# Left operands of seven feed forward units: transposed by TensorE, or made as rows and transposed by DMA

## The chip, the cores and the metric

The kernel runs on one core of one Trainium2 chip. The metric is the device time of one execution in microseconds. Before the change three runs gave 2137.55, 2141.11 and 2142.48 us, a median of 2141.11.

A core has TensorE (PE, the matrix engine), VectorE (DVE), ScalarE (ACT), GpSimd (POOL) and SyncE (SP), each with its own instruction stream that it runs in order. In this kernel SP issues nearly all transfers between the chip's memory and the on-chip SBUF; 16 DMA engines carry them. TensorE writes to PSUM, from where DVE and ACT read.

## The reference

One transformer-like block over x of shape (4, 1024, 2048), taken as 4096 rows of 2048:

```
mod = (silu(c) @ wmod).reshape(4, 6, 1, 2048)
sa, ca, ga, sb, cb, gb = mod[:, 0], ..., mod[:, 5]      # ga and gb are kept at least 0.25 from zero
h = layernorm(x) * (1 + ca) + sa
x = x + ga * (long convolution of h along 2048 + D[0] * h)
h = layernorm(x) * (1 + cb) + sb
x = x + gb * (h @ W.T + bias + sum_e w_e * (h @ A_e.T) @ B_e.T)      # w = coeffs * scales, 16 adapters
```

The change bears on the last two lines, the feed forward part: a modulated layer norm of x, and a 2048 x 2048 matrix product with the adapters merged into W.

## The kernel before

**Stages.** First come the modulation products (L317), the tables of the convolution, then 32 blocks of 128 rows through the convolution (`conv_mm`, L614), with the merging of the adapters into W between them (`merge`, L486 to L533). The result of a block, with the residual added, is written to memory as `x1d` (L656), and its mean and scale are kept in `ln2`. Then comes the feed forward part.

**Feed forward.** It works on 16 units of 256 rows (`NU`), and goes over them twice: pass q = 0 makes one half of the output columns, q = 1 the other (the loop at L1079 to L1108). A unit is a 2 x 2 block product by Strassen's scheme (Winograd's form): seven products in place of eight, in the order `ORDER = (0, 4, 5, 1, 6, 2, 3)`. Every operand is held as two half precision numbers, a high part and the remainder (`hl`), and a product takes three matmuls for each of eight chunks: 24 matmuls of 128x128 by 128x512 (`prod`, L750). ACT copies some products out of PSUM (L758), DVE combines them with the residual and the gate (L768 to L802), SP stores the output (L775). The PSUM banks X, Y and Z of a unit are each accumulated onto again later in the same unit: product 6 adds to the bank of product 5, product 1 to that of 0, product 2 to that of 4, product 3 to that of 6.

**Weights.** `load_w` (L980) loads the right operand of one product, 2 x 1 MB, and keeps it for a whole pass in `wc`. At the change of pass each is loaded anew, once the last unit's product has used the old one.

**Left operands.** `left` (L683) makes the seven left operands of a unit. It loads two 128x2048 tiles of `x1d`, normalizes them with ACT (L690), transposes them on TensorE, 32 transposes of 128x128 float32 per unit (L700), and ACT applies `cb` and `sb`, which in that layout are one number per partition, while it empties PSUM (L702). Then come the sums and differences of Strassen's scheme on DVE (L719 to L726), and for each operand `put`: ACT makes the high part (L712), DVE the remainder (L713), SP stores the pair to `lfd` (L714). In pass 0 the operand is used from SBUF where it was made; in pass 1 `left_load` (L731) brings it back from `lfd`. The pool `l` that holds the operands has 8 buffers, one operand of 512 KB each.

**What sets the order.** `left` is a generator. The function `tick` (L1098) is called after each product of a unit u and takes steps of the generator of unit u + 1 as `LPLAN` tells: the transposes come in groups of eight behind the first four products, then the sums, then the loads for unit u + 2. The recording layer orders each engine's stream by its own estimate of when things are ready, starting from the program's order, and puts in the waits. A transfer has one of eight completion semaphores in turn, so an SP transfer also waits until the eighth one before it has landed. Residual tiles `xo` come from the pool `o`, five buffers for four tiles per unit.

Of the kernel before, what the change touches and what calls it, by code (L numbers as in the profile page):

```python
# [12 lines left out]
F32 = mybir.dt.float32  # L13
F16 = mybir.dt.float16
# [5 lines left out]
MUL, ADD, SUB = ALU.mult, ALU.add, ALU.subtract  # L20
# [4 lines left out]
P = 128  # L25
D = 2048
# [8 lines left out]
class Net:  # L35
# [644 lines left out]

    def left(self, pl, u, res):  # L683
        nc, v = self.nc, self.nc.vector
        b = u // 4
        xs = []
        for r in range(2):
            x = pl["x2"].tile([P, D], F32, tag=f"x2{r}", name="x2")
            nc.sync.dma_start(out=x, in_=self.x1d[2 * u + r])
            nc.scalar.activation(  # L690
                x, x, AF.Identity, bias=self.ln2[:, 2 * u + r, 0:1], scale=self.ln2[:, 2 * u + r, 1:2]
            )
            xs.append(x)
        yield
        t = pl["t"].tile([P, NC, 2, P], F32, tag="t", name="gt")
        for c0 in range(0, NC, 2):
            tp = self.tps.tile([P, 2, 2, P], F32, tag="t", name="tp2")
            for c in range(2):
                for r in range(2):
                    nc.tensor.transpose(tp[:, c, r], xs[r][:, ds(P * (c0 + c), P)], self.ident)  # L700
            for c in range(2):
                nc.scalar.activation(  # L702
                    t[:, c0 + c], tp[:, c], AF.Identity,
                    bias=self.sb[:, c0 + c, b : b + 1], scale=self.cb[:, c0 + c, b : b + 1],
                )
            yield
        a11, a12 = t[:, 0:HC, 0, :], t[:, HC:NC, 0, :]
        a21, a22 = t[:, 0:HC, 1, :], t[:, HC:NC, 1, :]

        def put(i, s):  # L710
            hl = pl["l"].tile([P, HC, 2, P], F16, tag="l", name="lf")
            nc.scalar.copy(hl[:, :, 0, :], s)  # L712
            v.tensor_tensor(hl[:, :, 1, :], s, hl[:, :, 0, :], SUB)  # L713
            STQ(nc).dma_start(out=self.lfd[u, i], in_=hl)  # L714
            res[i] = hl

        put(0, a11)
        s = pl["s"].tile([P, HC, P], F32, tag="s", name="s")
        v.tensor_tensor(s, a21, a22, ADD)  # L719
        put(4, s)  # L720
        v.tensor_tensor(s, s, a11, SUB)
        put(5, s)
        put(1, a12)
        v.tensor_tensor(a21, a11, a21, SUB)
        put(6, a21)
        v.tensor_tensor(s, a12, s, SUB)  # L726
        put(2, s)
        put(3, a22)
        yield

    def left_load(self, pl, u, i):  # L731
        hl = pl["l"].tile([P, HC, 2, P], F16, tag="l", name="lf")
        self.nc.sync.dma_start(out=hl, in_=self.lfd[u, i])
        return hl

    def left_again(self, pl, u):
        return {i: self.left_load(pl, u, i) for i in ORDER}

    def ffn_unit(self, pl, u, q, lf, wc, tick):
        nc, v = self.nc, self.nc.vector  # L740
        ps = {}

        def prod(i, name):
            first = name not in ps
            if first:
                ps[name] = self.acc.tile([P, 512], F32, tag="a", name="f" + name)
            n = 0
            for k in range(HC):
                for x, y in ((0, 0), (0, 1), (1, 0)):
                    nc.tensor.matmul(  # L750
                        ps[name], lf[i][:, k, x, :], wc[i][k // 4][:, k % 4, y, :],
                        start=(first and n == 0), stop=(n == 3 * HC - 1), skip_group_check=True,
                    )
                    n += 1

        def copy(name, tag):
            t = pl["e"].tile([P, 512], F32, tag=tag, name=tag)
            nc.scalar.copy(t, ps[name])  # L758
            return t

        def at(x, r, h):
            return x[ds(P * r, P), ds(1024 * h + 512 * q, 512)]

        xs = {}
        for r, h in ((0, 0), (1, 1), (0, 1), (1, 0)):
            x = pl["o"].tile([P, 512], F32, tag="o", name="xo")
            nc.sync.dma_start(out=x, in_=at(self.x1d[2 * u : 2 * u + 2].rearrange("r p d -> (r p) d"), r, h))
            v.tensor_tensor(x, x, self.gbias[:, h], ADD)  # L768
            xs[r, h] = x

        def finish(r, h, cv, t):
            x = xs[r, h]
            v.tensor_tensor(t, cv, self.gbt[:, h], MUL)  # L773
            v.tensor_tensor(x, x, t, ADD)
            STQ(nc).dma_start(out=at(self.io["out"][ds(256 * u, 256), :], r, h), in_=x)  # L775


        prod(0, "X")
        p1 = copy("X", "p1")
        tick()  # L780
        prod(4, "Y")
        p5 = copy("Y", "p5")
        tick()
        prod(5, "Z")
        p6 = copy("Z", "p6")
        tick()
        prod(1, "X")
        finish(0, 0, ps["X"], pl["e"].tile([P, 512], F32, tag="p7", name="fin"))
        v.tensor_tensor(p6, p6, p1, ADD)
        tick()  # L790
        prod(6, "Z")
        p7 = copy("Z", "p7")
        v.tensor_tensor(p5, p5, p1, ADD)
        v.tensor_tensor(p7, p7, p5, ADD)
        finish(1, 1, p7, p7)
        tick()
        prod(2, "Y")
        v.tensor_tensor(p6, p6, ps["Y"], ADD)
        finish(0, 1, p6, p6)
        tick()  # L800
        prod(3, "Z")
        v.tensor_tensor(p1, p1, ps["Z"], ADD)  # L802
        finish(1, 0, p1, p1)
        tick()
# [5 lines left out]
MR = 2  # L810
ACC, TPS = 5, 2
PLAN = ("PNSL", "NL", "NSL", "NTL", "SL", "SL", "SL", "SL", "FSL", "SSL")
LPLAN = ("LL", "LL", "LL", "LL", "L", "0", "")
R0 = 5
WM, WMS = 3, 3
ROWC = 2700
# [7 lines left out]
def STQ(nc):  # L824
    return nc.sync
# [7 lines left out]
def net(ctx: ExitStack, tc: tile.TileContext, io):  # L833
# [3 lines left out]
    make_identity(nc, k.ident)  # L837
    k.x1d = k.dram.tile([32, P, D], F32, tag="x1d", name="x1d")
    k.ln2 = k.const("ln2", [P, 32, 2])
    k.lfd = k.dram.tile([NU, 7, P, HC, 2, P], F16, tag="lfd", name="lfd")  # L840

    def pool(stack, name, bufs, side="left"):
        return stack.enter_context(tc.tile_pool(name=name, bufs=bufs, side=side, reuse_waits="tile"))
# [37 lines left out]
    def take(g, n):  # L881
        for _ in range(n):
            next(g, None)
# [76 lines left out]
    def rest():  # L960
        mods = (x for sec in (4, 3, 5) for x in section(sec, (wmp,)))
        n = 0
        for _ in mer:
            yield
            n += 1
            if n % MR == 0:
                next(mods, None)
                yield
        for _ in mods:
            yield  # L970
        k.ginv = k.fold_scale(msm, k.cb, k.sb, "fs2", k.winv)
        yield

    fill = rest()
# [16 lines left out]

    def early():
        right.close()
        for name, bufs in (("w", 1), ("l", 8), ("t", 1), ("s", 1), ("x2", 1)):
            pr[name] = pool(p2, "p2" + name, bufs, "right")
        load_w(0, ORDER[0])

    def next_left(u):
        if u >= NU:
            return iter(())  # L1000
        lf[u] = {}
        return k.left(pr, u, lf[u])

    calls = [0]

# [63 lines left out]
        post = (r, xs.pop(r), *y)  # L1069
        nxt = follow[0] if follow else iter(())  # L1070
    k.conv_post(pl, *post)
    take(lgen, 10)
    gens = [next_left(1)]
    take(gens[0], 1)
    left.close()

    for name in ("v", "o", "e", "g"):
        pr[name] = pool(p2l, "p2" + name, 5 if name == "o" else 1)
    for q in range(2):  # L1079
        for i in ORDER:  # L1080
            if i not in wc or q == 1:
                load_w(q, i)
            if q == 1:
                lf.setdefault(0, {})[i] = k.left_load(pr, 0, i)
        for u in range(NU):
            b = u // 4
            if u % 4 == 0:
                ts_ = []
                for i in range(2):
                    t = pr["g"].tile([P, 2, 512], F32, tag=f"gb{i}", name=f"gb{i}")  # L1090
                    src = k.gbd[i][b].rearrange("(h n) -> h n", h=2)[:, ds(512 * q, 512)]
                    nc.sync.dma_start(out=t, in_=src.partition_broadcast(P))
                    ts_.append(t)
                k.gbt, k.gbias = ts_
                nc.vector.tensor_scalar(k.gbt, k.gbt, k.ginv[:, b : b + 1], None, MUL)
            plan = iter(LPLAN)

            def tick():  # L1098
                if q == 1:
                    return  # L1100
                for a in next(plan):
                    if a == "0":
                        gens[0] = next_left(u + 2)
                    take(gens[0], 1)

            k.ffn_unit(pr, u, q, lf.pop(u), wc, tick)
            if q == 1 and u + 1 < NU:
                lf[u + 1] = k.left_again(pr, u + 1)  # L1108
    p2l.close()
    p2.close()  # L1110

# [55 lines left out]
```

## Time and profile before

| what | value |
|---|---|
| median of three runs | 2141.11 us |
| the profiled execution | 2141.87 us |
| its span | 2140.1 us, mean granted TensorE clock 0.988 |
| first feed forward matmul | 918.9 us |
| last transpose of L700 | 1502.1 us |
| last feed forward matmul starts | 2134.2 us |
| moved by the DMA engines | 484.11 MB |
| products, L750 | 5376 matmuls, mean 379 ns of one (overlapping) |
| transposes, L700 | 512, mean 274 ns of one (overlapping) |
| PSUM to SBUF with cb and sb, L702 on ACT | 256, mean 576 ns |
| remainder of an operand, L713 on DVE | 112, mean 1219 ns |
| sum of two halves, L719 on DVE | 16, mean 1225 ns |
| residual plus bias, L768 on DVE | 128, mean 690 ns |

The page of a profile tells, for one execution, each engine's busy time and a picture of the span in 40 slices (a digit is the busy share in tenths). Behind it stand views that the trace answers: groups of instructions by line, who waited for whom, the instructions in order of time, and the busy time of all engines in a chosen stretch. Durations of matmuls and transposes overlap: the time that one costs is read from the distance between starts. The profile is of one execution, so sums made from it are set against that execution's own 2141.87 us.

### The profile page before, as it was taken

To read this page: it belongs to the slowest core of one execution; us is meant where nothing else is said; L and a number is where in the kernel's file an instruction comes from. 1 tells how busy PE (TensorE), PEld (TensorE's weight loads), DVE (VectorE), ACT (ScalarE), POOL (GpSimd) and SP (SyncE) were. 2 spreads that over 40 slices of the span, in tenths; PEclk is the share of its full clock that TensorE was granted. 3 is DMA by queue.
4 is the path that set the end of the run, shared out by engine and by line. 5 is a ranking of instruction groups with operands and counts; after the bars stand their busy time and mean duration, and the time that the engine had idled before them with its cause. 6 is when DMAs were issued, how large, how long until landed. Compare 5 with 4: busy or idle time off the path is not lost.

```text
span 2140.1 us, 28438 instructions
## 1 busy us (share of the span) xinstructions
PE 2082.4 (97%) x11113; PEld 1026.1 (48%) x11113; DVE 1308.4 (61%) x2353; ACT 923.7 (43%) x1695; POOL 6.3 (0%) x18
## 2 busy tenths in 40 slices
PE   7898999999999999999999999999999999999998
PEld 2344455555555555554545545555444444444444
DVE  5439898898979999665565565575533323332323
ACT  1325876677767777745454555555200000000000
POOL 0000000000000000000000000000000000000000
PEclk7999999999999999999999999999999999999999
DMA  9977566787776554387564564564794645454542
GB/s 401 373 307 278 225 227 265 285 310 262 276 278 227 187 192 173 139 346 258 190 241 180 202 240 179 203 235 172 283 341 163 192 151 167 164 170 165 177 157 69
DMA packets 127236, 484.11 MB, mean 226 GB/s; under 512 B 13608, under 2 KB 13768, under 8 KB 95998
## 3 DMA queue, kind: packets, MB, share of 16 engines
q1 hardware_dynamic: 126192, 477.55, 61.4%
q10 hardware_dynamic: 526, 2.63, 0.4%
q8 instruction: 87, 1.43, 0.3%
q0 software_dynamic: 384, 2.11, 0.2%
q14 instruction: 47, 0.39, 0.0%
HBM read 326.94 MB, written 155.30 MB: 225 GB/s over the span
## 4 chain that ended last, share of the span: by engine, by line
PE 67%; DVE 18%; ACT 6%; DMA 5%; issue 2%; SPq 0%; ACTq 0%; POOL 0%; DVEq 0%; POOLq 0%
PE fZ L750 22%; PE fY L750 15%; PE fX L750 15%; PE ya L614 5%; PE yb L614 3%; PE tp L700 3%; DVE wch L514 2%; PE modps L317 2%; DVE st L540 2%; DVE hc L593 2%; DVE y L641 2%; ACT x L660 2%; DMA wcd<-wch 1%; ACT t L582 1%; PE lps L486 1%
## 5 line engine op out<-in xcount | busy, mean ns | idle before, releaser
L750 PEld LDWEIGHTS <-lf 128*128 128x128 f16 x5376 | 526.0, 98 | 620.9 <-issue 1.4
L750 PE MATMUL fZ<-w,lf 128*128 128x512 f16 x2304 | 513.6, 379 | 0.8 <-ACT p L758 0.8
L750 PE MATMUL fX<-w,lf 128*128 128x512 f16 x1536 | 342.8, 379 | 0.0
L750 PE MATMUL fY<-w,lf 128*128 128x512 f16 x1536 | 342.0, 379 | 0.0
L614 PEld LDWEIGHTS <-hc 128*128 128x128 f16 x2304 | 215.3, 98 | 204.6 <-issue 41.6
L768 DVE TENSOR_TENSOR xo<-xo,gb 128x512 f32<-128x512 f32 x128 | 87.8, 690 | 238.7 <-DMA xo<-x1d 227.2
L582 ACT ACTIVATE t<-tp,sa,ca 128x128 f32<-128x128 f32 x480 | 188.1, 471 | 21.6 <-PE tp L578 12.9
L614 PE MATMUL ya<-kh,hs 128*128 128x512 f16 (+3 forms) x768 | 193.7, 326 | 3.7 <-DVE kh L284 2.6
L614 PE MATMUL ya<-kh,hc 128*128 128x512 f16 (+3 forms) x768 | 192.7, 328 | 3.8 <-ACT qs L627 3.6
L614 PE MATMUL yb<-kh,hc 128*128 128x512 f16 (+3 forms) x768 | 192.2, 327 | 1.8 <-DVE y L640 1.4
L758 ACT COPY p<-fZ 128x512 f32<-128x512 f32 x64 | 37.2, 581 | 286.8 <-PE fZ L750 272.1
L614 PEld LDWEIGHTS <-hs 128*128 128x128 f16 x1152 | 105.9, 98 | 108.6 <-issue 28.4
L758 ACT COPY p<-fX 128x512 f32<-128x512 f32 x32 | 18.7, 585 | 316.3 <-PE fX L750 210.4
L702 ACT ACTIVATE gt<-tp,sb,cb 128x256 f32<-128x256 f32 x256 | 124.9, 576 | 60.8 <-PE tp L700 60.8
L317 PE MATMUL modps<-wm,sct 128*32 128x512 f32 x768 | 118.8, 662 | 14.1 <-DMA wm<-in_wmod 14.1
L614 PE MATMUL ya<-kl,hc 128*128 128x512 f16 (+3 forms) x384 | 125.8, 328 | 0.0
L614 PE MATMUL ya<-kl,hs 128*128 128x512 f16 (+3 forms) x384 | 125.1, 326 | 0.7 <-DVE kl L285 0.7
L614 PE MATMUL yb<-kl,hc 128*128 128x512 f16 (+3 forms) x384 | 125.6, 327 | 0.0
L773 DVE TENSOR_TENSOR fin<-fX,gb 128x512 f32<-128x512 f32 x32 | 22.1, 692 | 128.4 <-PE fX L750 128.3
L593 DVE TENSOR_TENSOR hc<-t,hc 128x512 f16<-128x512 f32 x128 | 87.5, 684 | 6.6 <-ACT hc L592 6.4
L486 PE MATMUL lps<-lbh,lac 128*128 128x512 f16 x256 | 86.3, 379 | 1.2 <-DVE we L488 1.2
L578 PE MATMUL tp<-ident,n 128*128 128x128 f32 x512 | 79.3, 280 | 8.1 <-ACT t L582 6.3
(264 smaller groups left out, 2228.0 us busy)
## 6 DMA issues: line engine op xcount, KB each, us to landing
wm<-in_wmod SPq DMA_DIRECT2D x96, 1024.0 KB
lfd<-lf SPq DMA_DIRECT2D x112, 512.0 KB
lf<-lfd SPq DMA_DIRECT2D x112, 512.0 KB
x<-in_x SPq DMA_DIRECT2D x32, 1024.0 KB
x1d<-y SPq DMA_DIRECT2D x32, 1024.0 KB
x<-x1d SPq DMA_DIRECT2D x32, 1024.0 KB
xo<-x1d SPq DMA_DIRECT2D x128, 256.0 KB
out<-xo SPq DMA_DIRECT2D x128, 256.0 KB
```

The source lines that it names most:

```text
L317: self.last = self.nc.tensor.matmul(self.modps[32 * g : 32 * g + 32, :], self.sct[:, j].rearrange("p r b -> p (r b)"), w[:, ds(512 * g, 512)],
L486: nc.tensor.matmul(ps, la[:, x, k, h], y[:, k, osl], start=(n == 0), stop=(n == 5))
L514: v.tensor_tensor(hl[:, :, 1, :], tv, hl[:, :, 0, :], SUB)
L578: nc.tensor.transpose(tp[:, k], n[:, ds(P * (c0 + k), P)], self.ident)
L582: nc.scalar.activation(t[:, k], tp[:, k], AF.Identity, bias=self.sa[:, c, b : b + 1], scale=self.ca[:, c, b : b + 1],)
L593: v.tensor_tensor(lo[:, sl], src, hi[:, sl], SUB)
L614: nc.tensor.matmul(pf[:, o:512], h, self.kf[f][z][:, ds(k0, 512 - o)], start=first, stop=(i == last and (x, z) == (1, 0)), skip_group_chec ...
L700: nc.tensor.transpose(tp[:, c, r], xs[r][:, ds(P * (c0 + c), P)], self.ident)
L702: nc.scalar.activation(t[:, c0 + c], tp[:, c], AF.Identity, bias=self.sb[:, c0 + c, b : b + 1], scale=self.cb[:, c0 + c, b : b + 1],)
L750: nc.tensor.matmul(ps[name], lf[i][:, k, x, :], wc[i][k // 4][:, k % 4, y, :], start=(first and n == 0), stop=(n == 3 * HC - 1), skip_grou ...
L758: nc.scalar.copy(t, ps[name])
L768: v.tensor_tensor(x, x, self.gbias[:, h], ADD)
```

## The change

Units 2, 4, 6 to 14 (`BYDMA`) get another way to their left operands. `left_dma` normalizes the two tiles with ACT as before, and multiplies and adds the modulation on DVE while the rows are still rows; for this `mod_rows` writes `cb` and `sb` to memory as rows (`cbd`), and they come back broadcast over the 128 partitions (`cbr` once for four units, `sb` for each unit). The sums, the high parts and the remainders are made in that layout and stored to `lfd`. `left_load` then reads an operand with a transposing transfer, in both passes. In pass 0 the operands of these units thus come from memory, which they did not before. Units 0, 1, 3, 5 to 15 keep the transposes on TensorE (`left_pe`). The order of an operand in SBUF and memory is now high part first, then remainder.

Around it: `again` issues, after each product, the load of the operand that is used three products later (`LAG` = 4); the pool `l` has 7 buffers and `o` 3 in place of 8 and 5, the fourth residual of a unit is loaded after its first output is finished; the weights of pass 1 are loaded at the ticks of the last unit of pass 0; and `LPLAN` has one plan for units before a `left_pe` unit and one for those before a `left_dma` unit.

```diff
+    def mod_rows(self, pool):
+        nc = self.nc
+        self.cbd = self.dram.tile([2, NC, NB, P], F32, tag="cbd", name="cbd")
+        for i, t in enumerate((self.cb, self.sb)):
+            ps = self.tps.tile([NC * NB, P], F32, tag="t", name="cbp")
+            nc.tensor.transpose(ps, t.rearrange("p c b -> p (c b)"), self.ident)
+            row = pool.tile([NC * NB, P], F32, tag="mg0", name="cbr")
+            nc.vector.tensor_copy(row, ps)
+            nc.scalar.dma_start(out=self.cbd[i].rearrange("c b p -> (c b) p"), in_=row)
...
+    def left_pe(self, pl, u, res):
...
+        if u == 0 or u % 4 == 3 and u + 1 < NU:
+            self.cbr = pl["cb"].tile([P, NC, P], F32, tag="cb", name="cbb")
+            nc.sync.dma_start(out=self.cbr, in_=self.cbd[0, :, (u + 1) // 4, :].partition_broadcast(P))
...
+    def left_dma(self, pl, u):
+        nc, v = self.nc, self.nc.vector
+        b = u // 4
+        xs = self.left_rows(pl, u)
+        yield
+        t = pl["t"].tile([P, 2, D], F32, tag="t", name="gr")
+        sb, nl = t[:, 0], t[:, 1].bitcast(F16).rearrange("p (i x d) -> p i x d", i=2, x=2)
+        nc.sync.dma_start(
+            out=sb.rearrange("p (c d) -> p c d", d=P), in_=self.cbd[1, :, b, :].partition_broadcast(P)
+        )
+        yield
+        cb = self.cbr.rearrange("p c d -> p (c d)")
+        for row, op in ((cb, MUL), (sb, ADD)):
+            for x in xs:
+                v.tensor_tensor(x, x, row, op)
+                yield
+        a11, a12 = xs[0][:, 0:1024], xs[0][:, 1024:2048]
+        a21, a22 = xs[1][:, 0:1024], xs[1][:, 1024:2048]
+        n = [0]
+        def put(i, s):
+            hl = nl[:, n[0] % 2]
+            n[0] += 1
+            nc.scalar.copy(hl[:, 0], s)
+            v.tensor_tensor(hl[:, 1], s, hl[:, 0], SUB)
+            STQ(nc).dma_start(out=self.lfd[u, i], in_=hl.rearrange("p x d -> p (x d)"))
+        put(0, a11)
+        yield
...
     def left_load(self, pl, u, i):
-        hl = pl["l"].tile([P, HC, 2, P], F16, tag="l", name="lf")
-        self.nc.sync.dma_start(out=hl, in_=self.lfd[u, i])
+        hl = pl["l"].tile([P, 2, HC, P], F16, tag="l", name="lf")
+        if BYDMA(u):
+            self.nc.sync.dma_start_transpose(out=hl.rearrange("p x c r -> p (x c) r"), in_=self.lfd[u, i])
+        else:
+            self.nc.sync.dma_start(out=hl, in_=self.lfd[u, i].rearrange("p (x c r) -> p x c r", x=2, r=P))
         return hl
...
-        for r, h in ((0, 0), (1, 1), (0, 1), (1, 0)):
+        for r, h in ((0, 0), (1, 1), (0, 1)):
+            residual(r, h)
...
         finish(0, 0, ps["X"], pl["e"].tile([P, 512], F32, tag="p7", name="fin"))
+        residual(1, 0)
...
-LPLAN = ("LL", "LL", "LL", "LL", "L", "0", "")
+LPLAN = ("LL", "LL", "LL", "LL", "L0", "L", "LN"), ("LLLLL", "L", "LL", "L", "LL", "0", "")
+LAG = 4
+def BYDMA(u):
+    return u % 2 == 0 and u > 0
...
+    def again(n, j):
+        if j < LAG:
+            n, j = n - 1, j + 7
+        i, (q, u) = ORDER[j - LAG], divmod(n + 1, NU)
+        if q < 2 and (q or BYDMA(u)):
+            lf.setdefault((q, u), {})[i] = k.left_load(pr, u, i)
...
     for q in range(2):
         for i in ORDER:
-            if i not in wc or q == 1:
+            if i not in wc:
                 load_w(q, i)
-            if q == 1:
-                lf.setdefault(0, {})[i] = k.left_load(pr, 0, i)
...
             def tick():
-                if q == 1:
-                    return
-                for a in next(plan):
-                    if a == "0":
-                        gens[0] = next_left(u + 2)
-                    take(gens[0], 1)
+                j = len(done)
+                done.append(j)
+                if q == 0:
+                    for a in next(plan):
+                        if a == "0":
+                            gens[1] = next_left(u + 2)
+                        take(gens[a != "L"], 1)
+                    if u == NU - 1:
+                        load_w(1, ORDER[j])
+                again(q * NU + u, j)
```

## The prediction

> **What bounds the kernel now.** I read the page's busy rows and slices first, to see which engine sets the time.
>
> ```profile
> PE 2082.4 (97%) x11113; PEld 1026.1 (48%) x11113; DVE 1308.4 (61%) x2353; ACT 923.7 (43%) x1695; POOL 6.3 (0%) x18
> ...
> PE   7898999999999999999999999999999999999998
> ...
> DVE  5439898898979999665565565575533323332323
> ...
> PEclk7999999999999999999999999999999999999999
> DMA  9977566787776554387564564564794645454542
> ```
>
> TensorE is busy in every slice at full clock, so a busy share proves little: matmuls are pipelined. Whether PE really is the limit shows in the timeline of one unit of the first pass (start, us, engine, line):
>
> ```profile
> 1245.60 5.34 PE L750 MATMUL fY<-w,lf 128*128 128x512 f16 x24
> ...
> 1250.78 1.04 PE L700 MATMUL tp<-ident,x 128*128 128x128 f32 x8
> ...
> 1251.65 5.34 PE L750 MATMUL fZ<-w,lf 128*128 128x512 f16 x24
> ...
> 1263.76 5.34 PE L750 MATMUL fZ<-w,lf 128*128 128x512 f16 x24
> ...
> 1268.94 5.34 PE L750 MATMUL fY<-w,lf 128*128 128x512 f16 x24
> ```
>
> A product of 24 matmuls starts 5.18 us after the one before it (1263.76 to 1268.94), and 6.05 us after it where eight transposes stand between (1245.60 to 1251.65): eight cost 0.87 us of the stream, 109 ns each. The feed forward part runs from 918.9 to 2134.2: 32 x 7 x 5.18 = 1160.3 for the products, 15 units x 4 groups x 0.87 = 52.2 for the transposes, 1212.5 of 1215.3. It is PE, back to back, and what leaves PE there is gained unless something else becomes late. The stage view (length, busy time of PE, PEld, DVE, ACT, POOL, clock, DMA share, GB/s) tells what room the others have:
>
> ```profile
> 1200.00:1240.00 40.00, 40.00 (x203) 20.18 (x202) 23.59 (x29) 20.64 (x30) 0.00 (x0) 1.00 0.58 211
> ...
> 1520.00:1560.00 40.00, 40.00 (x187) 18.16 (x186) 12.11 (x19) 2.88 (x5) 0.00 (x0) 1.00 0.96 359
> ```
>
> A unit of the first pass takes 36.26 + 3.48 = 39.7 us; DVE has 16 us of it free and the DMA engines 42%. At the change of pass (second row) the DMA engines are full.
>
> **Part by part.** *Transposes.* Units 2, 4 to 14, seven of them, lose 32 each: 224 x 109 ns = **-24.4 us**, all on the path. The built order has 222 PE instructions fewer: 224 go, two come. Their 112 evictions (L702, 576 ns) leave ACT; it has slack, worth nothing.
>
> *DVE.* Rows need the modulation as four tensor operations of 128x2048 per unit: twice L719's 1225 ns, 2.45 us each, 9.8 us. By the built order one falls into the even unit before. In an odd unit DVE then has 3 x 2.45, seven splits of 1.22 (L713), four sums of 1.22 and 17 operations of 0.69: 32.5 us of 36.3. An even unit has 27.5 of 39.7. It fits. Followed through an odd unit in the built order with these durations, DVE ends 3.7 us into the next unit. It is in order, so its waits for residuals (L768, up to 6 us each here) delay what ACT copies. The tightest reader is PE's product 6, which accumulates onto the bank of product 5, whose ACT copy stands behind the first split: due at 20.7 us into the unit, done near 16.1. Cover 4.6 us; beyond it each microsecond of DVE delay is one of PE. I take 0.
>
> *Transposing loads.* 49 of 512 KB in each pass; those of the first pass are new traffic, those of the second replace plain loads. No row shows a transposing DMA. Nearest is the plain load lf<-lfd of the same bytes: 211 GB/s at a share of 0.58 is 364 GB/s when busy, 1.44 us. That is the lower end. The Trainium skill, page "DMA: Bandwidth & Descriptors", section "Latency and other measured facts", gives 261 GB/s for a transpose whose source rows aren't contiguous, as here (256 bytes out of 4 KB): 2.0 us, an estimate. A rule speaks against the change: "VectorE: DVE Perf Modes", section "The three transpose paths", prices a 128x128 block at 390 ns on TensorE and 1309 ns by DMA. The trace has 109 ns for TensorE, so by that rule the swap is twelve to one against DMA. Read as 16 blocks one after another, a load takes 20.9 us: the upper end. Read as 16 engines side by side it is 1.3 us. I take **2.0 us**, close to the nearest row.
>
> Its budget in the first pass: an odd and an even unit together move 2 x 8.1 MB as now (x 2.1, left operands 3.7, residual and output 1.05 each, gates 0.26), plus 1.6 MB of broadcast modulation rows: 17.8 MB, 48.9 us at 364 GB/s. The pair lasts 76.0 us. That leaves 27 us for seven loads, 3.9 us each; at 4.4 us the whole gain is gone. In the second pass 8.4 MB take 23 us of 72.5: 7.1 us each. At 2.0 us both hold: 0. At 20.9 us the pairs grow by 119 and 97 us, seven times each: 3630 us in all.
>
> *Lead.* With LAG 4 and seven buffers a load is issued two or more products ahead, 10.4 us. The tightest is the third one, issued on SP behind the last output of the unit before (about 3.7 us into the unit, as DVE above) with about 5 us of writes and an x load ahead of it in the ring: it lands near 11.7 with 2.0 us, and is needed at 12.1. At 3 us it would cost 0.6 a unit, 4 us in all. I take 0. Two residual buffers fewer lengthen SP's waits for outputs, which exist already and cover nothing on PE:
>
> ```profile
> SPq L767 <- DMA out<-xo: 183.2, 96, 5.6
> ```
>
> *Rows of cb and sb in the convolution part.* Two transposes and two copies of 64x128 (about 0.2 us each, like cb's 128x64 operation at 0.22), and two ACT stores. The second copy reuses the first one's buffer, so DVE waits for a store to land (an output lands 1.9 us after issue), and behind it stand PE's transposes for want of their two PSUM banks. 0.2 to 5, **+2**. The reshuffle of that part could also win 2.
>
> *Change of pass.* Before, SP issues weights i and left operand i in turn. After, operand i stands behind weights i+4, which wait for PE. Weights are 2.1 MB each, 5.8 us at 360 GB/s; with products ending every 5.18 us and outputs holding SP, operand 0 lands at about 38 us into unit 15 where 36.3 is needed, operands 1 and 2 slip by 1.5 and 2 more, and then the stream catches up. Bounds 0 (SP no later than before) and 10 (a full ring ahead of operand 2); **+5**, which is this count.
>
> Sum: -24.4 + 2 + 5 = -17.4 on the profiled execution's 2141.87 (span 2140.1 and 1.8 around it, 0.04% over the median of 2141.11): **2124 us**.
>
> **Rivals.** *Slow transposing loads.* Their source rows are cut into pieces of 256 bytes where the plain load reads 4 KB. From 4.4 us a load on, the DMA engines bound the first pass by more than PE gains, and the kernel is slower. At a quarter of the plain rate, 5.7 us: 48.9 + 39.9 = 88.8 against 76.0, +12.8 x 7 = 90, 2214 us. For it: no row bounds it, and the block price above. Against: the same section's 261 GB/s, and a share of 0.58 now.
>
> *DVE becomes the bound of odd units.* 32.5 of 36.3 busy, in order, behind residual loads. If waits put 3 us on each odd unit and the third load slips 0.6: 7 x 3.6 = 25: 2141.9 - 24.4 + 25 + 0.2 = 2143 with the sum's other terms at their low ends, no change; with 5 and 10 for them 2157. Against: even units have 12 us to recover.
>
> *The transposes leave PE, but the change of pass costs its 10 us and the convolution part 5:* 2133, inside the forecast's own range. That the change doesn't do its work is excluded by the instruction count.
>
> **Numbers.** Forecast 0.57, its own range 2114 to 2137; DVE or small stalls eating the gain 0.12 (2137 to 2157); slow loads 0.31, half of it below 2190. Low end: -24.4, nothing else lost, and 2 to 3 us won in the reshuffle. High end 2190, which leaves out the slower half of the last rival. 0.2% (4.3 us) is about what a measurement can tell from no change: faster 0.57, same 0.09, slower 0.34.
>
> **What would show it.** Products on PE 5.18 us apart in odd units, with no groups of transposes between; DMA share near 0.8 in the first pass; DVE near 32 us per odd unit; a PE gap of about 5 us near 1500 to 1560. It is wrong if PE waits for lf's loads in every even unit, or if the share is 0.95 or more from 1000 to 1500: then a load costs more than 3.9 us.

## The result and the profile after

The changed kernel takes **2236.2 us** (2231.7 to 2242.7, four runs) against 2140.3 for the kernel before in the same session, a ratio of 1.045 [1.042, 1.048]. Forecast were 2124 us, from 2114 to 2190. The profiled execution has a span of 2237.8 us, 97.7 over that of before.

The page's busy row and slices answer first:

```profile
PE 2089.0 (93%) x10891; PEld 1005.2 (45%) x10891; DVE 1370.7 (61%) x2383; ACT 874.1 (39%) x1583; POOL 6.2 (0%) x18
...
PE   6989999999999999988898988988989999999999
...
DVE  6439898889889997575655755657423233333333
...
PEclk8989999999999999999999999999999999999999
DMA  9986576778755463789788698796896565765663
```

The instruction count fell by 222, as the built order had it. From the eighteenth to the thirtieth slice (55.9 us each, 951 to 1678 us) TensorE shows 8s among its 9s: the loss is in the first pass of the feed forward part and at the change of pass. DVE shows no slice above 7 there: over such a stretch it is not full. The stage view places it (columns: stretch, length, then busy time of PE, PEld, DVE, ACT, POOL, clock, DMA share, GB/s):

```profile
1200.00:1240.00 40.00, 33.43 (x159) 16.37 (x158) 16.42 (x19) 20.27 (x29) 0.00 (x0) 0.91 0.98 265
...
1700.00:1740.00 40.00, 40.00 (x187) 18.13 (x186) 12.78 (x19) 2.34 (x4) 0.00 (x0) 1.00 0.69 168
```

Two things are lost in the first row: 6.6 us of PE, and clock (0.91). The second row is the second pass, with the same transposing loads, without a loss.

In what follows a rows unit is one of 2, 4, 6 to 14, whose operands are made as rows; they are made while the odd unit before it runs. While a rows unit runs, TensorE transposes x for the odd unit after it. PE's timeline of one such pair of units shows both losses (the bracket is idle time and what ended it):

```profile
1179.93 7.03 PE L821 MATMUL fZ<-w,lf 128*128 128x512 f16 x24 [3.79 <-ACT p L829]
...
1209.21 0.69 PE L721 MATMUL tp<-ident,x 128*128 128x128 f32 x2 [6.49 <-ACT x L702]
1209.69 7.43 PE L821 MATMUL fY<-w,lf 128*128 128x512 f16 x23
...
1270.63 5.34 PE L821 MATMUL fZ<-w,lf 128*128 128x512 f16 x24 [3.27 <-ACT p L829]
```

There are two gaps in a pair: product 6 of the odd unit waits for ACT's copy of product 5, and the next unit's transposes wait for a normalized x. The same wait comes back after 90.7 us (1179.93 to 1270.63), where a pair took 79.5 before (twice 36.26 + 3.48) and 76.0 was forecast. And after a gap the product can take 7 to 8 us for the same 24 matmuls. Over 919 to 1690 us PE is idle for 84.1 us (1.6 before), and products are 27.6 us longer than 5.34 us each. With 6.7 us more in the convolution part (first product at 925.65, before 918.93) and 24.4 us of transposes gone that is 82.5 + 27.6 + 6.7 - 24.4 = 92.4 of the 97.7; 5 us are not accounted for.

The waits of the first pass, 919 to 1640 us (who, for what, us in total, times, longest):

```profile
ACT gr L778 <- DVE x L769: 79.4, 7, 11.9
ACT x L702 <- DMA x<-x1d: 73.3, 23, 7.9
...
DVE x L769 <- DMA gr<-cbd: 54.4, 7, 8.8
ACT gr L778 <- DMA lfd<-gr: 48.5, 24, 5.7
...
PE tp L721 <- ACT x L702: 41.7, 8, 7.7
...
PE fZ L821 <- ACT p L829: 27.1, 8, 6.8
```

Read from the bottom, they form chains that lead back to a DMA. One of them in order of time, from the four engines' timelines:

```profile
1070.15 0.46 SPq L762 DMA_DIRECT2D gr<-cbd  x1
...
1081.65 2.29 DVE L769 TENSOR_TENSOR x<-x,gr 128x2048 f32<-128x2048 f32 x1 [8.38 <-DMA gr<-cbd]
...
1084.03 1.04 ACT L778 CAST gr<-x 128x1024 f16<-128x1024 f32 x1 [11.83 <-DVE x L769]
...
1084.98 0.58 ACT L829 COPY p<-fZ 128x512 f32<-128x512 f32 x1
1085.61 6.71 PE L821 MATMUL fZ<-w,lf 128*128 128x512 f16 x17 [3.67 <-ACT p L829]
```

(The last row ends where the view ends; the 24 matmuls of that product take 8.21 us.) The row of sb is issued at 1070.15 and not before: pool `t` has one buffer, and until then it holds the transposed rows from which the odd unit's own operands are made. It is used at 1081.65. DVE stands in front of it, ACT's first split stands behind DVE, the copy of product 5 stands behind the split, and PE stands behind the copy.

### The profile page after: what moved, and what is told of

Its sections match the earlier page's. It is cut to its first block, busy times and chain, and to the rows that moved or that the text cites. A ratio compares the mean times of both kernels' runs of the same rounds, so it can differ in the third digit from the quotient of the medians.

```text
span 2237.8 us, 28028 instructions
## 1 busy us (share of the span) xinstructions
PE 2089.0 (93%) x10891; PEld 1005.2 (45%) x10891; DVE 1370.7 (61%) x2383; ACT 874.1 (39%) x1583; POOL 6.2 (0%) x18
## 4 chain that ended last, share of the span: by engine, by line
PE 47%; DVE 23%; DMA 18%; ACT 7%; issue 4%; SPq 1%; POOL 0%; ACTq 0%; DVEq 0%; POOLq 0%
PE fZ L821 13%; PE fX L821 10%; PE fY L821 9%; PE ya L614 6%; DMA x<-x1d 4%; PE yb L614 3%; DMA gr<-cbd 3%; DMA xo<-x1d 2%; PE modps L317 2%; DVE wch L514 2%; DVE st L540 2%; DVE hc L593 1%; DMA wcd<-wch 1%; DMA w<-wcd 1%; DVE y L641 1%
## 5 line engine op out<-in xcount | busy, mean ns | idle before, releaser
L821 PEld LDWEIGHTS <-lf 128*128 128x128 f16 x5376 | 531.6, 99 | 689.6 <-issue 65.6
L821 PE MATMUL fZ<-w,lf 128*128 128x512 f16 x2304 | 528.6, 386 | 32.9 <-ACT p L829 27.1
L821 PE MATMUL fY<-w,lf 128*128 128x512 f16 x1536 | 353.9, 388 | 0.0
L702 ACT ACTIVATE x<-x,ln 128x2048 f32<-128x2048 f32 x32 | 67.0, 2094 | 73.3 <-DMA x<-x1d 73.3
L578 PE MATMUL tp<-ident,n 128*128 128x128 f32 x512 | 79.1, 279 | 11.5 <-ACT t L582 7.0
L540 DVE BATCH_NORM_STATS2 st<-x 128x6 f32<-128x512 f32 x128 | 84.0, 682 | 1.4 <-DMA x<-in_x 1.4
```

Source lines behind the costliest of these rows:

```text
L540: v.bn_stats(st[:, q], x[:, ds(512 * q, 512)])
L578: nc.tensor.transpose(tp[:, k], n[:, ds(P * (c0 + k), P)], self.ident)
L702: nc.scalar.activation(x, x, AF.Identity, bias=self.ln2[:, 2 * u + r, 0:1], scale=self.ln2[:, 2 * u + r, 1:2])
L821: nc.tensor.matmul(ps[name], lf[i][:, x, k, :], wc[i][k // 4][:, k % 4, y, :], start=(first and n == 0), stop=(n == 3 * HC - 1), skip_grou ...
```

## Experiments

Each run is compared with the kernel before on the same chip (2140.8 to 2145.1 us).

| version | median, us | ratio |
|---|---|---|
| plain loads | 2221.9 | 1.037 [1.035, 1.039] |
| no row of sb | 2212.2 | 1.033 [1.030, 1.035] |
| transposes later | 2251.3 | 1.050 [1.047, 1.054] |
| all by TensorE | 2167.2 | 1.012 [1.009, 1.014] |
| all by TensorE, loads as before at the change of pass | 2160.4 | 1.009 [1.007, 1.011] |
| all by TensorE, no rows of cb and sb | 2164.1 | 1.011 [1.009, 1.013] |
| operands reordered | 2237.6 | 1.045 [1.044, 1.047] |
| no row of sb, transposes later | 2223.5 | 1.039 [1.036, 1.041] |
| four split buffers | 2245.8 | 1.050 [1.047, 1.052] |
| stores on GpSimd | 2282.3 | 1.066 [1.062, 1.069] |
| four split buffers, stores on GpSimd | 2259.4 | 1.056 [1.053, 1.058] |
| three units | 2192.8 | 1.024 [1.021, 1.028] |
| no x, no row of sb | 2205.1 | 1.030 [1.027, 1.032] |
| short loop | 2254.7 | 1.052 [1.049, 1.055] |
| short loop, loads a product earlier | 2237.4 | 1.044 [1.042, 1.046] |
| x rows on GpSimd | 2251.7 | 1.051 [1.048, 1.053] |
| three removed | 2203.1 | 1.028 [1.026, 1.030] |
| four removed | 2170.5 | 1.014 [1.012, 1.015] |

**Plain loads.** The transposition is left out.

```diff
-            self.nc.sync.dma_start_transpose(out=hl.rearrange("p x c r -> p (x c) r"), in_=self.lfd[u, i])
+            self.nc.sync.dma_start(out=hl, in_=self.lfd[u, i].rearrange("p (x c r) -> p x c r", x=2, r=P))
```

> The 98 transposing loads are plain loads of the same 512 KB; the transposition is left out. If the buffer chains are the cause (the tiles t and x2 stay in use to the end of a unit made as rows, so the next sb row and the next x tile come late), PE still waits for ACT in both kinds of unit: 2195 us or more. If the transposing loads themselves are the cause (SP busy 2.6 us with each in place of 0.3, 256-byte packets), 2115 to 2145 us.

14 us less of 96: the rival I had given most weight, slow transposing loads, is only a part, as long as the other links stand. Whether these 14 are time on the 16 DMA engines ("the rings") or on SP was not separated. The stage view (changed kernel, then plain loads) answers another question, whether full rings hold PE:

```profile
1000.00:1500.00 500.00, 438.31 (x1985) 202.15 (x1985) 306.91 (x332) 189.48 (x235) 0.00 (x0) 0.94 0.83 238
1000.00:1500.00 500.00, 450.62 (x2065) 208.99 (x2065) 320.37 (x345) 199.83 (x246) 0.00 (x0) 0.95 0.72 248
```

A share of 0.83 over a pair of 90.7 us is 75 us of the 16 engines' time, against 45 before (0.56 of 79.5); in single stretches of 40 us the share reaches 1.0. With plain loads it is 64 us of a pair of 88, no such stretch from 1000 to 1600 us is above 0.85, and PE still idles for 71 us. So full rings are not what keeps the pair this long, but they are close behind.

**No row of sb.** The rows units add cb's row in place of sb's; sb is left out there.

```diff
-        nc.sync.dma_start(
-            out=sb.rearrange("p (c d) -> p c d", d=P), in_=self.cbd[1, :, b, :].partition_broadcast(P)
-        )
-        for row, op in ((cb, MUL), (sb, ADD)):
+        for row, op in ((cb, MUL), (cb, ADD)):
```

> The row of sb is not loaded, and cb's row is added in its place (sb is left out of these units). Buffer chains: the waits of product 6 on ACT's copy (27 us, doubled by the clock) go, the waits for x stay: 2190 to 2212 us. Transposing loads: seven transfers fewer of 105, within 10 us of 2236.

The waits of this run have

```profile
PE fZ L818 <- ACT p L826: 6.1, 6, 3.6
```

PE's wait for the copies falls from 27.1 to 6.1 us and the time by 24: the chain shown above is real. The wait for x stays (44.5 us).

**Transposes later**, by `LPLAN[0] = ("", "LL", "LLL", "LLL", "L0", "L", "LN")`.

> In even units TensorE's transposes for the next unit start behind the second product and not behind the first. Buffer chains: the waits for the normalized x tile (42 us and the clock behind them) mostly go: 2175 to 2205 us. Transposing loads: nothing in their number or place changes, so the wait moves elsewhere, within 15 us of 2236.

A miss: 15 us slower, with 39.4 us of waits for x still there. PE's wait for the copies grew to 32.9 us, which fits that later transposes also release tile t, and with it the row of sb, later.

**All by TensorE**: `BYDMA` returns False, so only the scaffold of the change is left (rows in the convolution part, smaller pools, the order of loads).

> No unit is made as rows; all the rest of the change stays (pools of 7 and 3, loads three products ahead, order at the change of pass, rows of cb and sb). Both theories: 2140 plus 3 to 10 at the change of pass and 0 to 4 in the convolution part, 2143 to 2154 us. Over 2160 would mean that the scaffold itself costs.

The scaffold alone costs 25 us, where the prediction had 7 for it. Its first product starts at 927.0, 8 us later than before. In the first pass PE has twelve waits of 0.2 to 0.9 us for ACT's copies, 5.3 in all, nearly all of them of a unit's last product; before there was one, of 0.8. Whether the fewer residual buffers bring them or the new order was not separated. At the change of pass PE has this:

```profile
1576.19 7.50 PE L821 MATMUL fX<-w,lf 128*128 128x512 f16 x24 [6.39 <-DMA w<-wcd]
1583.53 5.34 PE L821 MATMUL fY<-w,lf 128*128 128x512 f16 x24
1589.79 5.35 PE L821 MATMUL fZ<-w,lf 128*128 128x512 f16 x24 [0.92 <-DMA lf<-lfd]
```

Two runs split it:

```diff
                     if u == NU - 1:
                         load_w(1, ORDER[j])
+                        lf.setdefault((1, 0), {})[ORDER[j]] = k.left_load(pr, 0, ORDER[j])
```

> The version with every operand by TensorE (2167) with the first unit of the second pass loading its operands in the last unit of the first pass, each right behind the weights of the same product, as the kernel before does, in place of three products ahead. If the change of pass costs about 10 of the scaffold's 25 us there by its order of loads: 2154 to 2160. If the rings are simply full there whatever the order: 2164 to 2170.

```diff
-        k.mod_rows(msm)
-            self.cbr = pl["cb"].tile([P, NC, P], F32, tag="cb", name="cbb")
-            nc.sync.dma_start(out=self.cbr, in_=...)
```

> The version with every operand by TensorE (2167) without the two rows of cb and sb being transposed, stored and loaded, which nothing uses there. If these small steps hold up the convolution part by the 8 us that its end is late: 2157 to 2161, the first matmul of the feed forward part at 919 to 921 us in place of 927. If the 8 us come from something else (the smaller pools, the other order of the left operands): 2165 to 2169, first matmul still at 926 to 927.

The order of loads is worth 7 us in the median, and those waits of PE are gone from the trace; another of 4.4 us, for a copy by ACT, came in the same unit. The intervals of the two ratios overlap. Without the rows the first product is at 920.3, but only 3 us of median follow, within the intervals. The start of the first product doesn't measure the rows' cost: in the 18 profiles of versions that have the rows, TensorE, DVE and ACT run the same instructions in the same order up to it, and it starts anywhere from 914.8 to 927.0 us. What all 18 show is a wait of PE for the second copy, `cbr`, of 2.5 to 3.3 us, and 3 us is what the median gave.

**Looking for the link in the first pass.** The theory was a loop of single buffers over two units (transposes, tile t, row of sb, operands, x tile, transposes). Two edits that should shorten it, the operands in another order and the two earlier edits together:

```diff
-        put(1, a12)
         v.tensor_tensor(a21, a11, a21, SUB)
         put(6, a21)
+        put(3, a22)
+        put(1, a12)
         v.tensor_tensor(s, a12, s, SUB)
         put(2, s)
-        put(3, a22)
```

> The rows unit makes its operands in the order 1, 5, 6, 7, 4, 2, 3 of the products (a11, a21+a22, the next sum, a11-a21, a22, a12, the last sum) in place of 1, 5, 6, 2, 7, 3, 4, so that its second x tile is last read two operands earlier and its first tile before the last operand. Nothing else changes and the output is the whole computation. Theory of the loop of single buffers (x tiles, then tile t): the wait of the even units' transposes for the normalized x (41.7 us in the changed kernel) falls below 20 us and the median to 2190 to 2212. Rival, the transfers as such (the rings and the SP queue are full, and a wait that goes comes back elsewhere): 2225 to 2240.

> Two earlier edits together: the row of sb is not loaded (cb's row is added in its place, so sb is left out of the rows units), and the transposes of the even units are planned one product later. Alone they gave 2212 and 2251. Were they independent, 2225 to 2230 would follow. The theory of the loop (row of sb waits for tile t, the operands for the row, the next x for the operands, the transposes for x, tile t for the transposes) says that the later transposes failed alone because the row of sb closed the loop behind them; with the loop open here they should pay: 2170 to 2200, with the wait of transposes for x below 20 us.

Both missed. In the first of them the last x load is issued 5 us earlier in the first pair (1021.4 in place of 1026.3), but the pair stays at 91 us: the planner (the recording layer that orders each stream) now puts the even unit's transposes behind the whole second product (24 matmuls, then eight transposes), where they stood one to three matmuls into it, and both x tiles must be there at once. The second, no row of sb with transposes later, comes out near the sum of its parts (2225 to 2230).

The splits' own buffers were next, then SP's queue:

```diff
-        sb, nl = t[:, 0], t[:, 1].bitcast(F16).rearrange("p (i x d) -> p i x d", i=2, x=2)
+        sb = t[:, 0]
+        nl = [t[:, h].bitcast(F16).rearrange("p (i x d) -> p i x d", i=2, x=2)[:, i] for h in (1, 0) for i in range(2)]
-            hl = nl[:, n[0] % 2]
+            hl = nl[n[0] % 4]
```

> The rows unit's operands are split into four buffers in turn in place of two: the two of before and the half of tile t that held the row of sb, which is free once the row is added. The whole computation is kept. Reordering the operands and opening the loop through tile t had not shortened the pair of units (90 us in the changed kernel, 76 before), so the theory is now another: the split of an operand (ACT gr L778) waits for the store two operands earlier to have landed (48.5 us in 24 waits), which makes the seven operands take about 27 us where VectorE's part is 13, and with them the x tile comes free late. Theory of the two split buffers: those waits go, the transposes' wait for x falls from 41.7 to below 15 us, median 2185 to 2210. Rival, SP's queue in its order (the stores and the x loads stand behind transposing loads of 2 to 8 us each): 2222 to 2240, with the stores issued as late as before.

```diff
-            STQ(nc).dma_start(out=self.lfd[u, i], in_=hl.rearrange("p x d -> p (x d)"))
+            nc.gpsimd.dma_start(out=self.lfd[u, i], in_=hl.rearrange("p x d -> p (x d)"))
```

> The changed kernel with the rows unit's seven stores issued by GpSimd, which is idle in the feed forward part, in place of SP; two split buffers as in the changed kernel. Theory of the two split buffers: the store still has to land, its latency is a few us of ring and write whatever the queue, so 2215 to 2238 and ACT gr still waits for lfd<-gr. Rival, SP's queue in its order: 2185 to 2210, with the waits of ACT gr for lfd<-gr below 15 us.

With four buffers the split's wait for stores went from 48.5 us to 2.1, and the transposes' wait for x from 41.7 to 21.8. The time did not fall. PE's timeline of that run says why:

```profile
1200.99 0.69 PE L721 MATMUL tp<-ident,x 128*128 128x128 f32 x2 [3.83 <-ACT x L702]
1207.03 1.04 PE L822 MATMUL fY<-w,lf 128*128 128x512 f16 x2 [5.36 <-DMA lf<-lfd]
```

and its SP queue:

```profile
1195.76 0.45 SPq L701 DMA_DIRECT2D x<-x1d  x1
1196.31 8.58 SPq L806 DMA_TRANSPOSE lf<-lfd  x1
```

The planner moved the transposes one product ahead and took back what the earlier x gave. Then the second product waits for its own operand (42.3 us in 7 waits), whose transposing load stands in SP's queue behind the second x load and takes 8.6 us there. Stores on GpSimd made it worse (ACT's wait for them rose from 48.5 to 64.5 us), and both edits together gave 2259.4.

**Loop or each unit by itself?**

```diff
-    return u % 2 == 0 and u > 0
+    return u % 4 == 0 and u > 0
```

> The changed kernel with units 4, 8 and 12 alone by rows and DMA, and the other four by TensorE again. Against the version with none (2167) seven such units cost 69 us more, 9.9 each. If each unit is late by itself (its own row of sb, its own x behind its own operands): 2167 + 3 x 9.9 = 2197, from 2190 to 2203. If the lateness is that of a loop that closes every two units (one pair hands it to the next), a rows unit every four units leaves the loop some 150 us for its 90, and the cost per unit falls to 4 or less: 2160 to 2180.

8.5 us for each unit over the scaffold's 2167, against 9.9 with seven: the loop is out. A rows unit is late by itself.

The plan of the even units was also shortened, with four split buffers and with the second pass's first operands behind their weights, then with the transposing loads a product earlier (`LAG = 3`):

```diff
-LPLAN = ("LL", "LL", "LL", "LL", "L0", "L", "LN"), ...
+LPLAN = ("LLLL", "LLLL", "L", "L0", "L", "N", ""), ...
```

> Three edits that keep the whole computation: four split buffers as before; the even units' transposes planned over two products in place of four and their operands right behind, so that tile t comes free and the row of sb is loaded some 10 us earlier; and the operands of the second pass's first unit loaded right behind the weights (worth 7 us where every operand was by TensorE). Theory of the loop: the pair of units falls from 90 to about 80 us, 7 x 10 less, and 5 to 7 us at the change of pass: 2160 to 2185. If the loop does not set the pair's time (a throughput does): 2225 to 2245.

> As the one before, and transposing loads asked for four products ahead of their use in place of three. With four split buffers product 2 of the even units waited 42 us for its operand in all (7 waits), its load having been issued behind the next x loads in SP's queue. Theory of the loop: another 10 to 30 us off, 2140 to 2175. Rival (a throughput is short, or SP's queue is then held by loads whose stores have not landed): within 8 us of the one before, or slower.

Neither gained on the changed kernel (2254.7 and 2237.4), though the plan is shorter by two products. They prove less than the three units do: the first is slower than both of its ranges, with 61 us of PE's waits for `lf`, and the second is 17 us faster than the first, with 28 us of them. Asking for the loads one product earlier is worth those 17 us in this plan.

**Several links at once.** First the row of sb, by the edit shown above, and the x of the odd units from 3 on, both left out:

```diff
-        xs = self.left_rows(pl, u)
+        xs = self.left_rows(pl, u) if u < 2 else [self.cbr.rearrange("p c d -> p (c d)")] * 2
```

> The row of sb is not loaded (cb's row added in its place), and the odd units from 3 on transpose the resident row tile of cb in place of their own rows of x, so that these rows are neither loaded nor normalized: sb in the rows units and x in those odd units are left out. Two links of the chain are cut. Theory of the chain of waits: the first alone gave 2212; the 44 us of waits of transposes for x and the slow clock behind them (7 gaps of some 2.7 us) go too, which leaves 2150 to 2175. Rival, a throughput that is short (the 16 rings, or SP's issue of transposing loads): the time only moves to other waits, 2190 to 2210.

7 us over the run without the row of sb: a miss, and this run's queues tell why. SP, ACT and PE in order of time:

```profile
1277.63 6.09 SPq L802 DMA_TRANSPOSE lf<-lfd  x1
...
1284.40 7.65 SPq L802 DMA_TRANSPOSE lf<-lfd  x3
...
1292.11 1.05 SPq L701 DMA_DIRECT2D x<-x1d  x2
1297.86 2.09 ACT L702 ACTIVATE x<-x,ln 128x2048 f32<-128x2048 f32 x1 [12.91 <-DMA x<-x1d]
...
1301.40 2.03 PE L721 MATMUL tp<-ident,cbb 128*128 128x128 f32 x8 [7.87 <-ACT gt L723]
```

Four transposing loads hold SP for most of 14 us. The rows unit's x loads come behind them, ACT waits in order for that x, the evictions of the transposes stand behind it, and PE stops. These transposes need no x at all. So I gave the x rows, and those of cb and sb, to GpSimd's queue, in a version that keeps the whole computation and has four split buffers and the second pass's first operands behind their weights:

> The whole computation kept: the rows of x, of cb and of sb loaded by GpSimd's queue in the feed forward part, so that they don't stand behind SP's transposing loads (a run of four held SP for 14 us just ahead of the x loads), with four split buffers and the second pass's first operands right behind its weights. If SP's hold on the x loads is the link that takes over once the split buffers are four: 2175 to 2205, transposes' wait for x below 20 us. If the x loads are late because the tile is free late or the rings are full, as when the stores went to GpSimd (2282): 2230 or more.

A miss (2251.7): PE's wait for the copies grew to 63.1 us, from 27.1, and the transposes still wait 32.6 us for x. So it is not shown that SP's hold on the x loads costs time in the whole kernel. Last, the links removed together: plain loads, no row of sb and four buffers, then also no x of the odd units.

> Three things removed at once from the changed kernel: plain loads in place of transposing ones (the transposition of the rows units' operands is left out), no row of sb (cb's row added in its place, sb left out), four split buffers. Alone they gave 14, 24 and -10 us. If they are independent: 2236 - 28 = 2208. If they hide one another, since each is one link of the same late chain in front of the even units' transposes and the next link takes over when one is gone: clearly more than their sum, 2150 to 2190, and the wait of the transposes for x falls below 20 us. What stays above 2143 (the scaffold's 2167 less the 24 us of transposes) is then what no edit here has reached.

> As with three things removed (2203: plain loads, so the transposition is left out; no row of sb, so sb is left out; four split buffers), and the odd units from 3 on transpose the resident row tile of cb, so that their rows of x are neither loaded nor normalized and x is left out there. Cutting x had given 7 us where SP was still held by transposing loads. If what is left in the first pass (58 us of idle TensorE and 19 us of slow clock with three removed) is the chain of x tile, load and normalize: 2150 to 2175. If each link contributes for itself: about 2196. If it is 2196 or more, the rest sits in loads of the operands and in the order of the queues, and not in the making of the operands.

Three removed give 33 us, about the sum of what each gave alone (14 + 24 - 10 = 28). The fourth gives another **33**, where the same cut gave 7 with the other links in place. With four removed PE is idle for 35.0 us (84.1 in the changed kernel) and slow products cost 8.5 (27.6). So the x tile's chain and the removed three hide each other. How much of that is the transposing loads, and how much the split buffers, no run separates; none has the transposing loads in place and all other links removed. 27 us stay above 2143, the scaffold's 2167 less the 24 us of transposes. The scaffold has the gaps at the change of pass too (7.7 us, here 8.2), so they are not in the 27: its profile has 20 us more idle PE than the scaffold's (35.0 against 14.8), in the first pass.

No version here beats the kernel before.

## Why the prediction was wrong

The sum had +7 for the scaffold and -24.4 for the seven rows units. The version with all by TensorE has 25 for the scaffold, and the rows units add 69 to it: with the 24.4 that they save, their waits cost about 93 us, where the sum had nothing.

- *What bounds the kernel* and *transposes, -24.4*: these hold. 222 instructions left PE, and in the version with four links removed the balance comes within 4.4 us with them: 33.4 us more idle, 8.5 of slow products, 1.4 in the convolution part, less 24.4, is 18.9 of the 23.3 that its span is longer than that of before. They were only a small part of what happened.
- *DVE, 0*: the count was right (DVE is not the limit, rows 2.29 us against my 2.45), and I named the reader that broke: product 6 behind ACT's copy behind the first split, with a cover of 4.6 us. **What failed is that I followed DVE with its own durations and counted the row of sb as 1.6 MB of traffic, not as a wait.** Its tile is the one buffer t, so it can be issued only behind the last operand that is made from t for the odd unit, and it is 11.5 us from issue to use. In six odd units product 6 then waits 2.3 to 3.8 us beyond its cover; in the first one, unit 1, it is the last product that waits, 6.8 us for the copy of product 6. Taking the load away gave 24 us.
- *Missing altogether*: the x tiles. Before, an x tile is free once it is transposed; in a rows unit it is the operands' source until the last split. The next unit's load, 6 to 9 us, and two normalizations of 2.1 us come behind, and PE's transposes stand at a place fixed by the order. I looked at the lead of the operands, and not at the release of each buffer that the new path keeps longer. Cutting the x tile's chain gave 7 us with the other links in place and 33 as the last removal. SP's hold by transposing loads stands in one trace ahead of the x loads, but the version that should have shown its worth did not gain.
- *Transposing loads, 2.0 us, 0*: one is 2048 packets of 256 bytes with a mean of 21.6 ns, 2.77 us of the 16 engines, 190 GB/s beside the other traffic. That is under the budget of 3.9 us, and slower than the Trainium skill's 261 GB/s ("DMA: Bandwidth & Descriptors", "Latency and other measured facts"). The other rule I weighed ("VectorE: DVE Perf Modes", "The three transpose paths", 1309 ns per block by DMA) was far off in the other direction if blocks come one after another: 2.77 us for 16 of them. The budget was mis-sized as well: the sum had 48.9 + 7 x 2.0 = 63 us of the engines' time for a pair, and the pair has 75, with the rows' packets of 512 bytes and longer packets of everything else in it (those of 2048 bytes took 110 ns, 98 before). A pair of 76.0 us would have left next to nothing free. The rival of slow loads thus named a side that came true (slower) with a mechanism that is 14 us of it while the other links stand. That the result fell on its side is luck. What I did not price was the issue: a median of 2.6 us of SP, up to 8.0, against 0.33 for a plain load. I had priced none of the queue's time.
- *Rows in the convolution part, +2 (0.2 to 5)*: the mechanism was right, PE waits 3.0 us for the second copy, cbr, and so was the size. The rest of the 6.7 us lies within what profiles with the same order of instructions differ by (914.8 to 927.0).
- *Change of pass, +5 (0 to 10)*: waits of 5.7, 2.1 and 0.3 us and one slow product, 9.8 us in all: in the bounds, near the high end.
- *Two residual buffers fewer, 0*: with all by TensorE there are 5.3 us of small waits in the first pass; whether these buffers or the order bring them stays open.
- *Clock*: not in the sum. Each gap of PE can bring a slow product after it, 27.6 us in all.

The two signs I named beforehand (PE waiting for lf in every even unit; a DMA share of 0.95 from 1000 to 1500) did not come: PE waits for lf in two of seven, and the share is 0.83. That it is near the 0.8 that I forecast is luck: it is 75 us of a pair of 90.7, and would have been nearly 1 in the forecast pair of 76.0. The prediction failed on waits that I had not listed.

What stays open: how the 33 us divide between the x tile's release and the links that it hides, why PE's last waits, most of the 27 us above 2143, stay, and what the planner would have done with more room.

## What to carry to other kernels

When an operation moves from the limiting engine to a longer path, list every buffer that the new path holds and ask when each is released, and what is loaded into it next; a load whose bytes fit into the rings may still start too late. Read the queues that issue transfers as engines with durations. Where an order is planned, a relaxed link is often given back by the plan, and chains that run side by side hide one another: remove them together before calling one of them harmless.

## What the runs showed of the hardware

- A transposing load of 512 KB holds SP for 1.7 to 8.0 us (median 2.6; a plain one of the same size 0.33), and four in a row held it for 14.1 us; its packets are 256 bytes, 21.6 ns each on average.
- After an idle time of PE of some 2 to 8 us the next product of 24 matmuls often takes 6.6 to 8.3 us in place of 5.34, with weight loads 0.43 us apart (for 5.9 us in the product at 1085.61), and the granted clock of the 40 us around it is 0.83 to 0.96. It isn't every gap, and not by its length alone: 3.27 us was followed by 5.34, and 2.06 us by 7.04.
- A row of 8 KB spread to 128 partitions goes in packets of 512 bytes, 35.5 ns each on average: about 4.5 us of the 16 engines for 1 MB, and 11.5 us from issue to use in this load of the rings.
